# Token attention in a four-layer DiT: contraction in 128+128+32 channels, one transpose of maxima per unit, outputs packed to 96 rows, denominators per sequence

## The chip, the core and the metric

The kernel runs on one core of a Trainium2 chip. TensorE (PE) multiplies, VectorE (DVE), ScalarE (ACT) and GpSimd (POOL) work beside it, and SyncE (SP) issues nearly all DMAs, in the order of the program. The metric is the device time of one execution in microseconds; lower is better. All arithmetic is in float32.

## The reference

Four transformer blocks with adaptive layer norm are applied in turn to x, 4 sequences of 512 tokens with 288 channels. Each block is

```
mod  = silu(c) @ w_ada + b_ada                 # six vectors of 288 per sequence
h    = layernorm(x) * (1 + scale) + shift
q,k,v = split(h @ w_qkv + b_qkv)               # 16 heads of 18 channels
o    = softmax(q k^T / sqrt(18)) v
x    = x + gate * (o @ w_proj + b_proj)
h    = layernorm(x) * (1 + scale2) + shift2
x    = x + gate2 * mlp(h)                      # 288 -> 1152 -> 288, gelu
```

In layers 0, 1 and 3 the softmax runs over the 512 tokens of a sequence ("token attention"). In layer 2 it runs over the 16 heads of one token. Layer 0 has four experts in place of the MLP, two of them for each token. Biases are not zero.

## The kernel before

**Units and steps.** A token attention is cut into 16 units: 4 sequences times 4 groups of 4 heads. A unit has 4 steps, one for 128 tokens each, so there are 64 steps. `steps` (L729) writes the order out by hand. In step s the kernel computes, for four heads on four row groups of PE (32 rows each), the scores of the unit that is six steps ahead, only for their maxima over keys (`score`, L608; reduction on DVE, L660), and the scores of the current unit with the maxima already in them, transposed, so that ACT's exponential (L653) gives the weights at once. Two heads of each kind go in the first half of the step (`scores(step, 0)`), two in the second. Between the halves stands `sum_values` (L682): the weights of the step before, times values, summed into one PSUM bank over the unit's four steps. A column of ones among the values gives the denominator as a 19th row of each head.

**Two gaps.** After the sums and after the second half there is a `gap`: the place where other work is put in. Its argument is a number of microseconds by the program's own price list: `PACE = (0.3, 1.0)` (L526). Work is kept in four lists, sorted by the step in which each item is due: `products` (work for PE), `lanes` (norms and other chains), `loads` and `spreads` (DMAs). In a gap, an item is taken when what it reads is marked ready (`mark`, `ready`: counts of gaps, not times); with a budget of zero only items already due are taken. An item in `spreads` that yields WAIT keeps the list to itself until a later gap.

**Channels.** `chunks` (L486) turns the normed tokens, with channels on partitions, in three chunks of 96; the last has a 97th row of ones that carries the bias. `product` (L551) therefore needs three products for each output: `values(b, t)` four outputs of 128 x 288 per sequence, `queries_keys(b, m)` five outputs of 128 x 512 (the heads' queries and keys packed at 19 columns a head, 608 in all). Each result goes from its bank (6 or 7 in turn, `other`) to SBUF: L565 on DVE, L580 on ACT.

**Spread.** `spread(u)` (L598) copies the unit's queries and keys by 8 or more DMAs to one of four buffers `qk`, with 32 partitions for each head. It may run when the unit four earlier has used its buffer.

**Maxima.** `set_maxima(u)` (L664) turns the maxima, 128 x 4 for each of four token blocks, with four transposes (L668), copies 4 x 512 (L670), and writes each head's row into `qk` by a DMA (L672).

**Outputs.** Per unit, `denominators` (L693) turns the 128 x 512 sums with four transposes (L696), takes the reciprocals (L698), spreads them over 32 columns a head on POOL (L702); `normalise` (L706) turns them back with four transposes (L709) and multiplies on DVE (L712). `project` (L716, L719) multiplies four tiles of 128 rows, in which 18 rows of each 32 hold an output, with projection weights laid out the same way, for 128 tokens at a time; `add_gated` (L515, L516) adds the result to x.

**Around.** `load_attention` (L228) loads the weights by 32 small DMAs and two for the values; `scale_queries` (L272) scales the queries' weights on POOL. After a token attention come the expert blocks (layer 0) or the MLP, whose products have gaps of their own. The MLP for the first sequence of layer 1 runs inside the token attention, at step 48 (`early_mlp`). The MLP (`mlp`, L1575) already takes its channels as 128+128+32, the 32 of three outputs side by side in different rows of PE. Tiles live in pools with a fixed number of buffers by tag: `ot` has 7, `qc` 3, `rows` 1, `upd` 2.

Of the kernel before, what the change touches and what calls it, by code (L numbers as in the profile page):

```python
# [35 lines left out]
KF = 2  # L36
# [6 lines left out]
NQB = -(-NQ // P)  # L43
LEAD = 6
# [14 lines left out]
def tile_dit_blocks(ctx: ExitStack, tc: tile.TileContext, x_in, cond_t, sel_den, sel_b, w_gate, layers, out):  # L59
# [151 lines left out]
    mxs = [const.tile([P, TB, HG], F32, name=f"mx{i}") for i in range(2)]  # L211
# [16 lines left out]
    def load_attention(l):  # L228

        w, t = layers[l], w_att[l]  # L230

        wqk = wpool.tile([P, NK, NQ + C], F32, tag="wqk", name=f"wqk{l}")
        if l == OVER_HEADS:
# [3 lines left out]
        else:  # L237

            src = w["wqk"].rearrange("(k p) s (h d) -> p k s h d", p=KP, d=HP)
            bias = w["bqk"].rearrange("(o j d) s g -> o s g j d", o=1, d=HP)  # L240
            t["wqk"] = wqk[:, :, :NQ]
            wv = t["wv"] = wqk[:, :, NQ:]
            for g in range(NG):
                for s in range(2):
                    at = slice(g * UQ + s * HG * HO, g * UQ + (s + 1) * HG * HO)
                    for k in range(NK):
                        nc.sync.dma_start(
                            wqk[:KP, k, at].rearrange("p (j d) -> p j d", d=HO),
                            src[:, k, s, g * HG : (g + 1) * HG, :HO],
                        )  # L250
                    nc.sync.dma_start(
                        wqk[KP : KP + 1, NK - 1, at].rearrange("p (j d) -> p j d", d=HO), bias[:, s, g, :, :HO]
                    )
                if g == 0:
                    nc.sync.dma_start(wv[:KP], w["wv"].rearrange("(k p) f -> p k f", p=KP))
                    nc.sync.dma_start(wv[KP : KP + 1, NK - 1, :], w["bv"])
        mark(("loaded", l), 6)
        yield 0.0

    def load_projection(l):  # L260
        w, t = layers[l], w_att[l]
        wp = wpool.tile([P, NG, C], F32, tag="wp", name=f"wp{l}")
        t["wp"] = wp
        if l == OVER_HEADS:
            nc.sync.dma_start(wp[:KP, :NK, :], w["wp"].rearrange("(k p) f -> p k f", p=KP))
            nc.sync.dma_start(wp[KP : KP + 1, NK - 1, :], w["bp"])
        else:
            nc.sync.dma_start(wp, w["wp"].rearrange("(g p) f -> p g f", p=P))
# [3 lines left out]
    def scale_queries(l):  # L272

        for k in range(NK):
            n = KP + (1 if k == NK - 1 else 0)
            q = w_att[l]["wqk"][:n, k, :].rearrange("p (g s c) -> p g s c", g=NG, s=2)[:, :, 0, :]
            nc.gpsimd.tensor_scalar_mul(q, q, SCALE)
        mark(("weights", l))
        yield 0.2
# [61 lines left out]
    def mod_product(l, half, kinds):  # L341
# [13 lines left out]
        for kind in kinds:  # L355
            at = slice(kind * HP, kind * HP + B)
            nc.vector.tensor_tensor(row[at, :C], pr[at, :C], bada[at, :], ALU.add)
            if kind < 2 and half == 1 and l:
# [8 lines left out]
    def modulation(l, half, kinds=range(3)):  # L367
# [6 lines left out]
        if half == 0:  # L374
# [5 lines left out]
        if half == 0:  # L380
# [48 lines left out]
    def norm(l, half, b):  # L429
# [46 lines left out]
        elif half == 1:  # L476
# [9 lines left out]
    def chunks(l, half, b):  # L486
# [7 lines left out]
        for k in range(NK):  # L494
            if half == 0:
# [26 lines left out]
    def attention(l, start):  # L522
# [3 lines left out]
        PACE = (0.3, 1.0)  # L526
        qk, sums, done, ex, rec = {}, {}, {}, {}, {}
# [23 lines left out]
        def product(to, st, mv, us):  # L551

            for k in range(NK):
                rows = slice(0, KP + (1 if k == NK - 1 else 0))
                nc.tensor.matmul(to, st(rows, k), mv(rows, k), start=k == 0, stop=k == NK - 1)  # L555
                if k < NK - 1:
                    yield us

        def values(b, t):
            pv = other()[:, :C]  # L560
            h = ht[l, 0, b]
            yield from product(
                pv, lambda r, k: h[r, k, t * P : (t + 1) * P], lambda r, k: w["wv"][r, k, :], 0.48
            )
            nc.vector.tensor_copy(heads(vas[0])[:, t, :, :HD], pv.rearrange("p (h d) -> p h d", d=HD))  # L565
            count(b)
            yield 0.48

        packed = {}

        def queries_keys(b, m):

            h = ht[l, 0, b]
            n = min(P, NQ - m * P)
            pq = other()
            yield from product(
                pq[:n, :], lambda r, k: w["wqk"][r, k, m * P : m * P + n], lambda r, k: h[r, k, :], 0.86
            )
            t = packed[b, m] = work.tile([P, S], F32, tag="qc", bufs=3, name=f"qc_{l}_{b}_{m}")
            nc.scalar.copy(t[:n, :], pq[:n, :])  # L580
            mark(("packed", l, b, m), 1)
            count(b)
            yield 0.86
# [30 lines left out]
        def only_maxima(step):  # L614
# [7 lines left out]
            for j in range(HG):  # L622
                nc.vector.tensor_reduce(mxs[u % 2][:, c, j : j + 1], pm[j], AX.X, ALU.max)
# [16 lines left out]
        def scores(step, half):  # L640
# [16 lines left out]
            if maxima:  # L657
                for j in range(2):
                    h = 2 * half + j
                    nc.vector.tensor_reduce(mxs[mu % 2][:, mc, h : h + 1], pm[j], AX.X, ALU.max)  # L660
# [3 lines left out]
        def set_maxima(u):  # L664

            pm = other()
            for c in range(TB):
                nc.tensor.transpose(pm[:HG, c * P : (c + 1) * P], mxs[u % 2][:, c], ident)  # L668
            t = work.tile([P, S], F32, tag="qc", bufs=3, name=f"maxima_{l}_{u}")
            nc.scalar.copy(t[:HG, :], pm[:HG, :])  # L670
            for j in range(HG):
                nc.sync.dma_start(qk[u][j * HP + ONE : j * HP + ONE + 1, 0, :], t[j : j + 1, :])  # L672
            yield 0.5
# [19 lines left out]
        def denominators(u):  # L693
            pd = other()
            for c in range(TB):
                nc.tensor.transpose(pd[:, c * P : (c + 1) * P], done[u][:, c * P : (c + 1) * P], ident)  # L696
            r1 = small.tile([P, TB, HG, 1], F32, tag="r1", name=f"r1_{l}_{u}")
            nc.vector.reciprocal(  # L698
# [1228 lines left out]
```

## Time and profile before

| | |
|---|---|
| time, median of 3 runs | 2484.43 us (2483.38 to 2485.16) |
| the profiled execution, its span | 2486.91 us, 2485.2 us |
| token attention of layer 0, from the first score to the last copy of sums | 62 to 482 us |
| expert blocks | 488 to 928 us |
| token attention of layer 1 (with the early MLP) | 929 to 1369 us |
| MLP of layer 1, layer 2 | to 1945 us |
| token attention of layer 3 | 1946 to 2314 us |
| MLP of layer 3 | to 2485 us |
| TensorE's granted clock, mean | 0.943 |

How to read the profile: a row gives the line of the kernel, the engine, the operation, the tiles written and read, their shapes, and how often; then busy time, the mean of one instruction, and the idle time ahead of it with what ended it. A float32 product is two MATMUL rows. Products are pipelined, so the time that one takes from PE is read from the starts of two neighbours and not from its duration. In order of time, each row gives its start and length, both in us, and how many instructions were merged. The rows of a stretch give the busy us of PE, of its weight loads, of DVE, ACT and POOL, each with a count, then PE's granted clock, the share of the DMA engines and GB/s.

### The profile page before, as it was taken

The page shows a single profiled execution, that of the slowest core. Times are in us where ns is not written, and L with a number is a line of the kernel's source. Part 1 is how long each engine was busy: PE and PEld are TensorE (multiplying, and loading weights), DVE is VectorE, ACT ScalarE, POOL GpSimd, SP SyncE. Part 2 cuts the span into 40 slices and gives each one's busy share as a digit, 9 for nine tenths or more (in the row PEclk, how much of TensorE's full clock was granted, in tenths as well). Part 3 has the DMA queues.
Part 4 walks back from the last instruction along what each step waited for, and adds up shares of the span by engine and source line. Part 5 has one row for each costly group of instructions (what it writes and reads, how often), then busy time and mean ns, then how long its engine had stood idle before and what let it go on. Part 6 is the DMA issues. An engine that isn't in the chain of part 4 may idle for free. (4 is left out here: it accounts for less than half of the span.)

```text
span 2485.2 us, 30140 instructions
## 1 busy us (share of the span) xinstructions
PE 2291.2 (92%) x11188; PEld 1218.6 (49%) x11188; DVE 1086.3 (44%) x1955; ACT 834.8 (34%) x1233; POOL 521.4 (21%) x517
## 2 busy tenths in 40 slices
PE   5899999899998999999999999778589999999998
PEld 2333333367776773333353677455456433333455
DVE  2445655441012025555524669989210455555100
ACT  1244434422221223344426233323223244444311
POOL 2000020321022111100010257778621100011000
PEclk9699999999999997899999899888799799999999
DMA  5201110446554541000000001100110000000000
GB/s 143 97 30 62 38 36 12 107 161 189 177 160 152 175 124 62 13 14 16 28 21 1 22 3 32 36 17 17 22 56 2 28 16 16 14 14 6 1 20 20
DMA packets 163033, 134.23 MB, mean 54 GB/s; under 512 B 81365, under 2 KB 146725, under 8 KB 162886
## 3 DMA queue, kind: packets, MB, share of 16 engines
q1 hardware_dynamic: 159814, 122.86, 17.0%
q0 software_dynamic: 3072, 9.44, 1.2%
q8 instruction: 89, 1.46, 0.2%
q14 instruction: 58, 0.48, 0.1%
HBM read 90.67 MB, written 26.25 MB: 47 GB/s over the span
## 5 line engine op out<-in xcount | busy, mean ns | idle before, releaser
L660 DVE TENSOR_REDUCE mx<-banks 128x1 f32<-128x512 f32 x696 | 447.8, 685 | 370.9 <-PE banks L608 370.3
L608 PE MATMUL banks<-qk 32*128 32x512 f32 x3072 | 548.8, 681 | 11.8 <-DVE mx L660 7.0
L653 ACT ACTIVATE ex<-banks 128x1024 f32<-128x1024 f32 x348 | 356.4, 1024 | 513.2 <-PE banks L608 511.9
L608 PEld LDWEIGHTS banks<-qk 32*128 32x128 f32 x3072 | 180.5, 194 | 230.6 <-DVE mx L660 97.7
L863 POOL TENSOR_TENSOR pv<-hs,qk 128x1152 f32<-128x1152 f32 x64 | 203.7, 3196 | 50.2 <-DVE ho L875 35.3
L682 PE MATMUL banks<-ex,va 128*32 128x512 f32 x1536 | 212.2, 623 | 0.0
L1462 PE MATMUL banks<-w_b,hid_b 128*128 128x288 f32 x684 | 187.6, 417 | 0.0
L555 PE MATMUL banks<-ht,wqk 96*128 96x512 f32 (+1 forms) x360 | 186.7, 629 | 0.6 <-DVE upd_a L515 0.6
L1650 PE MATMUL banks<-ht,w 128*128 128x256 f32 x504 | 134.3, 402 | 38.2 <-ACT hid L1661 37.6
L1442 PE MATMUL banks<-block,w_b 128*128 128x256 f32 x684 | 165.8, 387 | 3.6 <-DMA w_b<-in_w 2.9
L702 POOL COPY rec<-r 128x512 f32<-128x512 f32 x48 | 29.6, 616 | 659.9 <-DVE r L698 586.2
L1672 PE MATMUL banks<-w,hid 128*128 128x288 f32 x504 | 151.8, 437 | 0.0
L1454 ACT ACTIVATE hid_b<-banks,b_b 128x256 f32<-128x256 f32 x171 | 68.7, 473 | 241.1 <-PE banks L1448 163.1
L1462 PEld LDWEIGHTS banks<-w_b,hid_b 128*128 128x128 f32 x684 | 123.9, 191 | 49.9 <-issue 21.9
L1442 PEld LDWEIGHTS banks<-block,w_b 128*128 128x128 f32 x684 | 129.3, 193 | 31.2 <-issue 11.4
L1650 PEld LDWEIGHTS banks<-ht,w 128*128 128x128 f32 x504 | 98.8, 201 | 61.7 <-ACT hid L1661 41.9
L719 PE MATMUL banks<-wp,ot 128*128 128x288 f32 x384 | 118.9, 435 | 5.9 <-DVE upd_a L515 3.5
L1672 PEld LDWEIGHTS banks<-w,hid 128*128 128x128 f32 x504 | 93.4, 198 | 46.3 <-issue 26.3
L516 POOL TENSOR_TENSOR x<-x,upd_a 128x288 f32<-128x288 f32 x48 | 38.1, 793 | 364.6 <-DVE upd_a L515 337.1
L555 PEld LDWEIGHTS banks<-ht,wqk 96*128 96x128 f32 (+1 forms) x360 | 61.4, 189 | 100.1 <-issue 86.2
L719 PEld LDWEIGHTS banks<-wp,ot 128*128 128x128 f32 x384 | 68.6, 195 | 76.1 <-issue 51.9
L682 PEld LDWEIGHTS banks<-ex,va 128*32 128x32 f32 x1536 | 31.1, 109 | 152.4 <-issue 150.6
(224 smaller groups left out, 2574.9 us busy)
## 6 DMA issues: line engine op xcount, KB each, us to landing
w_b<-in_w SPq DMA_DIRECT2D x57, 432.0 KB
w_b<-in_w SPq DMA_DIRECT2D x57, 384.0 KB
qk<-qc SPq DMA_DIRECT2D x336, 38.0 KB
wa<-in_wada SPq DMA_DIRECT2D x7, 864.0 KB
block<-x_mem SPq DMA_DIRECT2D x19, 288.0 KB
y_mem<-y_b SPq DMA_DIRECT2D x19, 288.0 KB
x_mem<-zeros SPq DMA_DIRECT2D x7, 768.0 KB
y_mem<-zeros SPq DMA_DIRECT2D x7, 768.0 KB
```

Source lines behind the costliest of these rows:

```text
L555: nc.tensor.matmul(to, st(rows, k), mv(rows, k), start=k == 0, stop=k == NK - 1)
L608: nc.tensor.matmul(to, qk[u][r, of, c * P : (c + 1) * P], qk[u][r, 1 - of, :], start=True, stop=True)
L653: nc.scalar.activation(e, WEIGHTS, AF.Exp)
L660: nc.vector.tensor_reduce(mxs[mu % 2][:, mc, h : h + 1], pm[j], AX.X, ALU.max)
L682: nc.tensor.matmul(SUMS[j * HP : (j + 1) * HP, :], vas[0][:, c, at : at + HP], ex[step, j // 2][:, j % 2, :], start=c == 0, stop=c == TB - 1,)
L719: nc.tensor.matmul(pp, done[b * NG + g][:, t * P : (t + 1) * P], w["wp"][:, g, :], start=g == 0, stop=g == NG - 1)
L863: nc.gpsimd.tensor_tensor(prod, sc[i][:, hs, :].unsqueeze(2).to_broadcast([P, GH, HD, NH]), qkv[i][:, 1].rearrange("p h d -> p d h").unsqu ...
L1442: nc.tensor.matmul(banks[:, UP + j, :BT], w1[:, k, j * P : (j + 1) * P], hx[i][:, k, :], start=k == 0, stop=False)
L1454: nc.scalar.activation(t, banks[:, UP + j, :BT], AF.Gelu_apprx_tanh, bias=b1[:, f : f + 1])
L1462: nc.tensor.matmul(banks[:, PY + t, :C], hid[j][:, t * P : (t + 1) * P], w2[:, j, :], start=f == 0, stop=f == NF - 1)
L1650: nc.tensor.matmul(banks[:, UP + j, :BT], full[:, k, (f % 3) * P : (f % 3 + 1) * P], h[:, k, s], start=k == 0, stop=False,)
L1672: nc.tensor.matmul(banks[:, PY + t, :C], hf[:, t * P : (t + 1) * P], w["w2"][f // 3][:, f % 3, :], start=False, stop=f == NF - 1,)
```

## The change

The token attentions of layers 0, 1 and 3 take channels as 128+128+32. The last 32 channels are held two more times below (32 to 63, 64 to 95), and two outputs are computed together (`products_of`), so that their remainders run side by side in different rows of PE; both outputs hold a bank until the end. Row 64 of the third weight chunk keeps the biases; at the start of a layer they are turned to columns and spread over partitions (`spread_biases`) and are added when a bank is emptied. The maxima are stored by head and block, so that one transpose of 16 columns does for a unit. When a unit's sums are copied, DMAs pack its heads, 18 rows each, into three tiles with 96 rows a sequence, and the denominators into 16 rows of the last (`gather_heads`). Once in a sequence the denominators are turned, inverted and turned back, written to memory, and read back over 18 rows a head by DMAs, in two groups; POOL multiplies. The projection takes three tiles. The first gap's budget is zero. The early MLP takes its hidden chunks in pairs.

```diff
-    mxs = [const.tile([P, TB, HG], F32, name=f"mx{i}") for i in range(2)]
+    mxs = [const.tile([P, HG, TB], F32, name=f"mx{i}") for i in range(2)]
...
     def load_attention(l):
...
+            chunk = [(k * P, P, 0, k) for k in range(KF)] + [(KF * P, RC, i * RC, KF) for i in range(2)]
             for g in range(NG):
                 for s in range(2):
-                    for k in range(NK):
+                    for c0, n, r0, k in chunk:
                         nc.sync.dma_start(
...
     def load_projection(l):
...
-            nc.sync.dma_start(wp, w["wp"].rearrange("(g p) f -> p g f", p=P))
+            for h in range(NH):
+                for k, r, at, n in parts_of(h):
+                    nc.sync.dma_start(wp[r : r + n, k, :], w["wp"][h * HP + at : h * HP + at + n, :])
+            nc.sync.dma_start(wp[KP : KP + 1, NK - 1, :], w["wp"][ONE : ONE + 1, :])
...
+    def spread_biases(l):
+        t = w_att[l]
+        row = t["all"][BIAS : BIAS + 1, KF, :]
+        pb = other()
+        for m in range(NQB):
+            n = min(P, NQ - m * P)
+            nc.tensor.transpose(pb[:n, m : m + 1], row[:, m * P : m * P + n], ident[BIAS : BIAS + 1, BIAS : BIAS + 1])
...
+        nc.tensor.matmul(pb, ones[BIAS : BIAS + 1, :], row[:, NQ:], start=True, stop=True)
+        t["bv"] = wpool.tile([P, C], F32, tag="bv", name=f"bv{l}")
+        nc.scalar.copy(t["bv"], pb)
...
-        PACE = (0.3, 1.0)
+        PACE = (0.0, 1.0)
...
+        def products_of(b, *which):
+            h = ht[l, 0, b]
+            jobs = []
+            for kind, i in which:
+                bank = other()
...
+            for kind, i, bank, product in jobs:
+                for k in range(KF):
+                    product(slice(0, P), k, k == 0, False)
+                    yield 0.48 if kind == "t" else 0.86
+            for j, (kind, i, bank, product) in enumerate(jobs):
+                product(slice(j * RC, (j + 1) * RC), KF, False, True)
...
         def set_maxima(u):
             pm = other()
-            for c in range(TB):
-                nc.tensor.transpose(pm[:HG, c * P : (c + 1) * P], mxs[u % 2][:, c], ident)
-            t = work.tile([P, S], F32, tag="qc", bufs=3, name=f"maxima_{l}_{u}")
-            nc.scalar.copy(t[:HG, :], pm[:HG, :])
+            n = HG * TB
+            nc.tensor.transpose(pm[:n, :P], mxs[u % 2].rearrange("p j c -> p (j c)"), ident)
+            t = small.tile([HG * TB, P], F32, tag="tops", bufs=1, name=f"tops_{l}_{u}")
+            nc.scalar.copy(t, pm[:n, :P])
...
-        def denominators(u):
...
+        def gather_heads(u):
+            b, g = divmod(u, NG)
...
+            for j in range(HG):
+                h = g * HG + j
+                for k, r, at, n in parts_of(h):
+                    nc.sync.dma_start(oc[b][k][r : r + n, :], done[u][j * HP + at : j * HP + at + n, :])
+                nc.sync.dma_start(last[KP + 1 + h : KP + 2 + h, :], done[u][j * HP + ONE : j * HP + ONE + 1, :])
+            mark(("packed heads", l, u), 2)
+            yield 0.0
+        def reciprocals(b):
+            pd = other()
+            rows = slice(KP, P)
+            for c in range(TB):
+                nc.tensor.transpose(
+                    pd[:, c * HP : (c + 1) * HP], oc[b][NK - 1][rows, c * P : (c + 1) * P], ident[rows, rows]
+                )
+            r1 = rec[b] = small.tile([P, TB, HP], F32, tag="r1", bufs=1, name=f"r1_{l}_{b}")
+            nc.vector.reciprocal(r1, pd[:, :P].rearrange("p (c h) -> p c h", c=TB))
+            mark(("reciprocals", l, b), 1)
+            yield 0.5
+        def reciprocal_rows(b):
...
+            nc.scalar.copy(t, pd[:HP, :])
+            mark(("reciprocal rows", l, b), 0)
...
-        def normalise(u):
+        def normalise(b):
+            rows = dram.tile([HP, S], F32, tag="rec", name=f"rec_rows_{l}_{b}")
+            nc.sync.dma_start(rows, rec[b])
+            room = {}
+            for ks in ((0, 1), (2,)):
+                t = work.tile([P, TB, C + 1], F32, tag="rows", bufs=1, name=f"by_{l}_{b}_{ks[0]}")
...
+                            nc.sync.dma_start(
+                                room[k][r : r + n, :], rows[1 + h : 2 + h, :].to_broadcast([n, S])
+                            )
+                for _ in range(3):
+                    yield WAIT
+                for k in ks:
+                    nc.gpsimd.tensor_tensor(oc[b][k][:KP, :], oc[b][k][:KP, :], room[k][:KP, :], ALU.mult)
+            mark(("outputs", l, b), 2)
+            yield 0.0
...
-                    products, at_step(last if b + 1 == B else last + (7 if l == 0 else 11) + t),
+                    products, at_step(last + 5 + t), [("outputs", l, b), ("gate", l, 0), ("projection", l)], project(b, t)
...
-                task(products, at_step(s + TB + 3), [("sums", l, u)], denominators(u))
-                task(products, at_step(s + TB + 5), [("reciprocals", l, u)], normalise(u))
+                free = [("x", l, 1, b - 1)] if b and not g else [("packed heads", l, u - 1)] if u else []
+                task(spreads, at_step(s + TB + 1), [("sums", l, u)] + free, gather_heads(u))
+            task(products, at_step(last + 2), [("packed heads", l, b * NG + NG - 1)], reciprocals(b))
+            task(products, at_step(last + 3), [("reciprocals", l, b)], reciprocal_rows(b))
+            task(spreads, at_step(last + 3), [("reciprocal rows", l, b)], normalise(b))
...
-        mlp(1, 0, b, TRIOS, home="hm")
+        mlp(1, 0, b, DUOS, home="hm")
```

## The prediction, on record before the result was known

> **What bounds the kernel now.** I read the page first, then the busy times by stretch, then PE's instructions in order of time inside the third token attention, where the clock is steady, then the DMA queue of SP.
>
> ```profile
> PE 2291.2 (92%) x11188; PEld 1218.6 (49%) x11188; DVE 1086.3 (44%) x1955; ACT 834.8 (34%) x1233; POOL 521.4 (21%) x517
> ...
> 2100.00:2200.00 100.00, 97.28 (x585) 34.99 (x588) 55.19 (x100) 47.47 (x55) 7.61 (x11) 1.00 0.05 16
> ```
>
> PE is busy 97.3 of 100 us there, DVE 55 and ACT 47: PE sets the pace, so fewer PE instructions should shorten the stage. Two stretches of the same layer show how far. First two full steps, then steps with no other product between the scores:
>
> ```profile
> 2157.32 1.14 PE L608 MATMUL banks<-qk 32*128 32x512 f32 x8
> 2158.39 1.06 PE L682 MATMUL banks<-ex,va 128*32 128x512 f32 x8
> 2159.38 1.12 PE L555 MATMUL banks<-ht,wqk 96*128 96x512 f32 x2
> 2160.44 1.14 PE L608 MATMUL banks<-qk 32*128 32x512 f32 x8
> 2161.51 1.99 PE L555 MATMUL banks<-ht,wqk 96*128 96x512 f32 x4
> 2163.43 1.14 PE L608 MATMUL banks<-qk 32*128 32x512 f32 x8
> 2164.50 1.06 PE L682 MATMUL banks<-ex,va 128*32 128x512 f32 x8
> 2165.49 0.66 PE L709 MATMUL banks<-ident,rec 128*128 128x128 f32 x4
> ...
> 2002.47 1.07 PE L682 MATMUL banks<-ex,va 128*32 128x512 f32 x8
> 2003.46 3.71 PE L608 MATMUL banks<-qk 32*128 32x512 f32 x16
> 2007.10 1.07 PE L682 MATMUL banks<-ex,va 128*32 128x512 f32 x8
> ```
>
> Start to start, one step is scores 1.07, sums 0.99, scores 1.07: 3.13 us of PE. The rest is products in two gaps: after the sums, and after the second scores. But the empty step takes 2007.10 - 2002.47 = 4.63 us: its two scores in a row need 3.64 instead of 2.14, because the second must wait for ACT's exponentials (1.02 us each) and DVE's maxima. So **the second gap holds 1.5 us of products for nothing**; what is removed below that returns nothing, although PE looks busy throughout. The ACT copies of the sums (L690) start at 1990.90 and, seven units later, at 2148.65: 22.5 us a unit of four steps, 90 a sequence of four units. 16 x 3.13 = 50 plus the 38 us of products of which I count the parts below agrees.
>
> **What the change removes from PE, per sequence.** An instruction below is one row of the trace; a float32 product is two of them, a transpose one.
> - Queries and keys: four instructions in 1.92 us (2161.51 to 2163.43), so 0.96 for a product. 15 become 13 (two pairs of 4 and one shared remainder; one of 3): -1.9. The remainder's two products run in different rows: three such took 17.0/15 = 1.13 us in the MLP (L1594), so 0.15 dearer than one: -1.6.
> - Values: L555 with 288 columns, 6 instructions in 1.65, 0.55 a product; 12 become 10: -1.1, with remainders -0.8.
> - Projection, same 0.55: 16 become 12: -2.2.
> - Transposes: 48 (maxima 16, sums 16, reciprocals 16) become 12; four take 0.6 (2165.49 to the next): 36 x 0.15 = -5.4.
>
> Together -10.0 us, times 12 sequences **-120 us**. It also takes 3.3 us of DVE work per sequence away (L712 688 ns, L698) and the POOL copies (616 ns); neither engine is late, so nothing is counted.
>
> **What comes back.** The order follows from due steps, so I placed the remaining 28 us of products per sequence step by step (second gap of step 0 for the values, 8 to 10 and 12 to 13 for the next queries and keys, 6 and 7 for the projection).
> - *Unfilled gaps.* About a third of the second gaps then hold under 1.5 us: 3 us lost per sequence in layer 3, also the short waits for both banks that a pair holds (evacuations L580 585 ns, L565 455 ns). Nine inner sequences: **+27** (bounds 0 to 45). In the last sequence of a layer no later products fill, and units there are 19.8, 16.7, 12.0 us already: 4.3 of the 10.0 is lost, **+13** (5 to 25).
> - *The wait for gathered rows.* The first reciprocal's transposes stand two gaps after the gather is issued. SP issues the spread of a later unit (9 DMAs, 588 ns each) just before, as its buffer comes free one step earlier; the gather is 8 DMAs.
>
> ```profile
> 2158.03 2.44 SPq L672 DMA_DIRECT2D qk<-maxima  x4
> 2167.31 7.59 SPq L598 DMA_DIRECT2D qk<-qc  x9
> 2180.62 2.43 SPq L672 DMA_DIRECT2D qk<-maxima  x4
> ```
>
>  6 us, then 8 x 0.56 = 4.5, then 1 to landing: 11.5 us after the sequence's end, while PE gets there after two steps, 9.3. That is 2.2; where the earlier gap is filled, 0.7. I take 1.3: nine times, **+12** (0 to 30). Behind PE's wait stand the next scores, so ACT and DVE wait too.
> - *Clock after a wait.* Around a wait for a DMA in layer 0 the granted clock fell:
>
> ```profile
> 410.00:425.00 15.00, 14.55 (x58) 5.52 (x50) 6.19 (x19) 4.73 (x7) 0.00 (x0) 0.66 0.07 20
> ```
>
>  15 us at 0.66 cost 5 us. With some such waits new, **+5** (0 to 25). The Trainium skill, "TensorE: Matmul & The Clock Gate", section "Why this matters for your kernels", asks for no idle gap over about 3 us; by it my shorter waits cost no clock and the sum would be 5 us better. The row above, where PE's shown wait was 0.45 us, speaks against leaving the term out.
> - *Ends of the three layers.* After the last step nothing hides the path: gather 4.5 + 1, copies, write of the reciprocals 0.36 plus about 2 to landing, 12 broadcasts, POOL's two products of 512 columns (L863 gives 2.77 ns a column: 1.4 each), 6 more broadcasts, one more product. A broadcast lies between L332 (272 ns) and L598 (588): I take 0.35, the row L1401 that also repeats a row of memory. That is 6 + 16 us against gaps of about 1.1 us (layers 0 and 1) or 2 us (layer 3) of MLP products, two and eight of them: PE waits about 8, 8 and 4, **+20** (6 to 45).
> - *Start and small things.* Layer 0 starts late by the 11 more weight DMAs (L247 477 ns, L255 321): 5 us, and first scores wait for SP today (18 spreads from 44.85 to 61.4, scores at 61.69); with the longer projection load and the pair's later evacuation 7. Spreading the biases 1.3 us a layer, MLP pairs instead of trios two remainders: **+13** (5 to 25).
>
> Sum: -120 + 27 + 13 + 12 + 5 + 20 + 13 = **-30 us**. The profiled execution took 2486.9 (span 2485.2 and 1.7 around it), so 2457; the median shown lies 2.5 below it: **2454 us**. With the bounds of the terms, all at once, -104 to +75; terms are independent, so I call 2425 to 2479 this case's own range.
>
> **Rivals.**
> - *Slower: SP's queue decides.* Per sequence SP issues 36 spreads and 16 maxima, 33.8 us by such spans (4 x (6.0, as most units have it, + 2.44)). Added are 34 gathers, 18 broadcasts and a write: 19.2 + 4.9 to 10.6 + 0.4. So 58 to 64 us of an 80 us sequence, in order, with waits for landing (2 us) and for POOL's 2.8 in it. Behind those stand the next maxima; today their last issue ends 8.6 us before their unit (2160.47 to the scores at 2169.06), and a gather and the broadcasts together are 9 to 12. From 0.6 us of wait per unit (30/48) on, the gain is gone; at 1.1 us the time is 2486.9 - 30 + 53 - 2.5 = 2507. For it: one queue at 75%, two long runs a sequence. Against: the maxima are known three steps before they are needed. The Trainium skill, "DMA: Bandwidth & Descriptors", section "Rules for kernel authors", says transfers under 64 KB pay mostly overhead; at the about 2 us it fits per DMA (another path), 53 would be an estimated 106 us a sequence and this case certain, but here four take 2.43.
> - *Much faster: everything is hidden.* If waits, clock and layer ends cost their lower bounds, -120 + 0 + 5 + 0 + 0 + 6 + 5 = -104; half way to it from -30, -67: 2417. For it: DVE and ACT are half idle. Against: the 4.63 us step.
> - *No change:* the terms cancel within 5 us, 0.2%, about what a measurement of this kernel can tell from no change.
>
> **Chances.** The forecast 0.42; much faster 0.14; no change 0.09; slower 0.35. So faster 0.56, same 0.09, slower 0.35. The range 2400 to 2515 leaves out half of the much faster case and a third of the slower one, 0.19.
>
> **What would show it.** PE instructions fall by about 4 x 3 x (4 + 4 + 8 + 36), 620, less some biases. Unit distances in layer 3 go from 22.5 to about 21.6 us: at 20 the much faster case holds, at 23 SP. New rows would be PE's waits for the gathered tile and for outputs, together 12 + 20 us; a wait of L608 for maxima over 30 us (1.0 today) would show SP deciding. I am wrong most easily in the place of the remaining products, which I derived from due steps and not from an order I could see.

## The result, and the profile after

The changed kernel takes **2654.12 us** (median of 4 runs, 2652.55 to 2663.76); the kernel before, run beside it, 2483.9 us. The ratio is 1.0696, 95% interval 1.0672 to 1.0721: 7% slower. The forecast was 2454, the range 2400 to 2515. Of the cases written down, the rival in which SP's queue decides comes nearest; it gave 2507.

The page's first row, then the stretch of layer 3 that was shown of the kernel before, and short stretches inside and just after it; in these rows the granted clock stands third from the end:

```profile
PE 2302.6 (87%) x10681; PEld 1218.6 (46%) x10681; DVE 1057.6 (40%) x1886; ACT 828.2 (31%) x1248; POOL 547.7 (21%) x517
```

```profile
2100.00:2200.00 100.00, 90.99 (x463) 30.27 (x460) 47.12 (x75) 41.34 (x47) 0.00 (x0) 0.89 0.07 20
2200.00:2208.00 8.00, 6.89 (x27) 1.89 (x27) 2.25 (x3) 1.28 (x2) 0.00 (x0) 0.50 0.01 3
2208.00:2212.00 4.00, 4.00 (x20) 1.30 (x20) 1.29 (x2) 1.02 (x1) 0.00 (x0) 0.98 0.00 0
2244.00:2251.00 7.00, 6.88 (x21) 2.15 (x22) 0.35 (x1) 1.83 (x3) 0.00 (x0) 0.50 0.07 20
2254.00:2260.00 6.00, 6.00 (x32) 3.14 (x29) 3.04 (x5) 2.93 (x4) 0.55 (x1) 1.00 0.09 22
```

PE has 507 instructions fewer, and is busy longer (2302.6 against 2291.2 us). It is busy 91 of 100 us where it was 97, and the clock is at half speed in two short stretches. PE's waits, each with its total in us, the number of times and the longest one:

```profile
PE banks L765 <- DMA oc<-ot: 52.6, 10, 8.4
PE banks L1514 <- DMA block<-x_mem: 41.8, 3, 22.2
...
PE banks L654 <- DMA qk<-tops: 35.1, 10, 7.6
```

L765 is the transpose of the gathered denominators, L654 the scores (L608 before), L1514 a block of the MoE layer. In the kernel before, the wait for the block was 4.3 us and that for the maxima 1.0; the first had no counterpart. Two of these waits, PE's instructions in order of time, a few rows each (idle time and its end in brackets):

```profile
2200.37 0.60 PE L765 MATMUL banks<-ident,oc 32*128 32x32 f32 x4 [5.56 <-DMA oc<-ot]
2200.91 0.38 PE L714 MATMUL banks<-ident,mx 128*16 128x128 f32 x1
2202.03 2.08 PE L605 MATMUL banks<-ht,wqk 128*128 128x512 f32 x2 [0.74 <-DVE r L769]
2204.03 2.09 PE L654 MATMUL banks<-qk 32*128 32x512 f32 x8
2206.05 1.94 PE L731 MATMUL banks<-ex,va 128*32 128x512 f32 x8
...
2212.05 1.07 PE L731 MATMUL banks<-ex,va 128*32 128x512 f32 x8
```

```profile
2244.12 2.63 PE L654 MATMUL banks<-qk 32*128 32x512 f32 x4 [7.43 <-DMA qk<-tops]
```

After the wait of 5.56 us the same eight products of the sums take 1.94 us, and 1.07 six microseconds later. So such a wait is paid twice: once itself, and once in the half clock behind it. SP's queue around them:

```profile
2184.28 5.84 SPq L644 DMA_DIRECT2D qk<-qc  x9
2190.42 0.77 SPq L756 DMA_DIRECT2D oc<-ot  x1
...
2198.37 0.54 SPq L757 DMA_DIRECT2D oc<-ot  x1
...
2223.60 0.37 SPq L786 DMA_DIRECT2D rec_rows<-rec  x1
2231.55 9.06 SPq L796 DMA_DIRECT2D by<-rec_rows  x18
2240.65 2.96 SPq L718 DMA_DIRECT2D qk<-tops  x4
```

The gather's eight DMAs (L756, L757) stand behind a spread and take 8.5 us to issue, not 4.5. The maxima of the next unit (L718) stand behind 18 broadcasts; the scores that need them wait 7.43 us.

Where the 166.8 us between the two spans lie, by the starts of the copies of the sums (a unit's end; L690 before, L739 after), in us:

| stage | before | after | products alone (e1) | outputs alone (e2) |
|---|---|---|---|---|
| start, to the first unit's end | 129.3 | 149.6 | 149.8 | 135.3 |
| the three token attentions, first to last unit's end | 1071.2 | 1161.0 | 1076.3 | 1155.2 |
| between layers 0 and 1 | 490.2 | 523.4 | 510.5 | 489.4 |
| between layers 1 and 3 | 622.8 | 643.3 | 634.9 | 631.5 |
| after the last unit | 171.8 | 174.7 | 171.8 | 175.3 |
| half clock in all | 285 | 521 | 347 | 435 |

"Half clock" is the time in which the trace's record of the granted clock says 0.5. 236 us more of it can cost up to 118 of the 167 us.

### The profile page after: what moved, and what is told of

It is laid out like the page before. It is cut to its first block, busy times and chain, and to the rows that moved or that the text cites. A ratio compares the mean times of both kernels' runs of the same rounds, so it can differ in the third digit from the quotient of the medians.

```text
span 2652.0 us, 29951 instructions
## 1 busy us (share of the span) xinstructions
PE 2302.6 (87%) x10681; PEld 1218.6 (46%) x10681; DVE 1057.6 (40%) x1886; ACT 828.2 (31%) x1248; POOL 547.7 (21%) x517
## 5 line engine op out<-in xcount | busy, mean ns | idle before, releaser
L654 PE MATMUL banks<-qk 32*128 32x512 f32 x3072 | 658.0, 704 | 56.3 <-DMA qk<-tops 35.1
L654 PEld LDWEIGHTS banks<-qk 32*128 32x128 f32 x3072 | 244.1, 201 | 380.3 <-issue 167.9
L731 PE MATMUL banks<-ex,va 128*32 128x512 f32 x1536 | 227.0, 661 | 0.0
L802 POOL TENSOR_TENSOR oc<-oc,by 96x512 f32<-96x512 f32 x36 | 45.4, 1261 | 860.4 <-DMA by<-rec_rows 859.4
L605 PE MATMUL banks<-ht,wqk 128*128 128x512 f32 (+1 forms) x360 | 170.6, 653 | 5.3 <-DVE r L769 3.7
L1561 PEld LDWEIGHTS banks<-w_b,hid_b 128*128 128x128 f32 x684 | 125.1, 192 | 49.7 <-issue 21.1
L1553 ACT ACTIVATE hid_b<-banks,b_b 128x256 f32<-128x256 f32 x171 | 69.1, 473 | 226.4 <-PE banks L1547 131.7
L1772 PEld LDWEIGHTS banks<-w,hid 128*128 128x128 f32 x504 | 93.0, 197 | 46.3 <-issue 26.1
L946 DVE TENSOR_TENSOR pq<-banks,qk 128x1152 f32<-128x1152 f32 x64 | 86.1, 1346 | 41.2 <-issue 21.8
L605 PEld LDWEIGHTS banks<-ht,wqk 128*128 128x128 f32 (+1 forms) x360 | 54.1, 194 | 91.4 <-issue 80.2
L473 DVE BATCH_NORM_STATS2 st<-x 128x6 f32<-128x288 f32 x128 | 56.2, 439 | 99.8 <-POOL x L1785 80.1
L952 DVE TENSOR_REDUCE hs<-pq 128x64 f32<-128x1152 f32 x64 | 86.6, 1353 | 14.5 <-POOL pv L962 11.7
```

What stands on the lines that cost most here:

```text
L605: nc.tensor.matmul(bank[:n, :], w["wqk"][r, k, i * P : i * P + n], h[r, k, :], start=start, stop=stop)
L654: nc.tensor.matmul(to, qk[u][r, of, c * P : (c + 1) * P], qk[u][r, 1 - of, :], start=True, stop=True)
L731: nc.tensor.matmul(SUMS[j * HP : (j + 1) * HP, :], vas[0][:, c, at : at + HP], ex[step, j // 2][:, j % 2, :], start=c == 0, stop=c == TB - 1,)
L946: nc.vector.tensor_tensor(prod, QUERIES[i % 2][:, :C].rearrange("p (h d) -> p h d", d=HD)[:, hs, :].unsqueeze(2).to_broadcast([P, GH, NH, ...
L952: nc.vector.tensor_reduce(sc[i][:, hs, :], prod, AX.X, ALU.add)
L1561: nc.tensor.matmul(banks[:, PY + t, :C], hid[j][:, t * P : (t + 1) * P], w2[:, j, :], start=f == 0, stop=f == NF - 1)
```

## The experiments

Ratios are to the kernel before, run beside it on the same chip. That took 2480 to 2493 us on these occasions, so runs are compared by their ratios: a difference of 0.01 between two ratios is 25 us of 2484. First the two halves of the change, and the issuing engine of two groups of DMAs.

**e1, the products' part.** The output path (`denominators`, `normalise`, `project`, `load_projection` and their tasks) is that of the kernel before.

> The changed kernel with the output path of the kernel before (denominators and products with them per unit, 128-row heads, the weights of the projection in one DMA); paired products, biases, the one transpose of maxima and the pace are the change's. Theory (SP's queue: gathers, write and broadcasts of the denominators stand in front of the maxima): without them SP has room again, the PE work of the products and of 12 maxima transposes per sequence, 4.2 us x 12 = 50 us, is gone and at most part of it comes back as empty gaps and a longer start: 2430 to 2480 us, the wait of the scores for the maxima under 3 us. Rival (the paired products, their two held banks or the empty first gap cost more than they save): over 2520 us.

2543.9 us, 1.0247 (1.0230 to 1.0264). The theory fails here: without the new DMAs there is still a loss of 2.5%. The wait for the maxima is 15.4 us, under half of that after the change but not under the 3 us expected. By the table the sequences gain nothing, and start and stages between the layers lose 53 us.

**e2, the outputs' part**, on the kernel before (`gather_heads`, `reciprocals`, `reciprocal_rows`, `normalise`, `project`, `load_projection` and their tasks).

> The kernel before with the change's output path alone (heads packed to 96 rows by gathers, denominators per sequence, broadcasts through DRAM, projection over three chunks); products, maxima and pace as before. Theory (SP's queue): as slow as the whole change or nearly so, 2570 to 2700 us, with waits of scores or reciprocals for DMAs of over 50 us in all and half-clock time over 400 us. Rival (the products are what costs): 2420 to 2500 us.

2590.36 us, 1.0440 (1.0422 to 1.0457): as expected of the queue. The two halves add up: 2.5% and 4.4% against 7.0%.

**e3, the output DMAs on GpSimd.**

```
-   nc.sync.dma_start(...)      # gather_heads, normalise
+   nc.gpsimd.dma_start(...)
```

> The changed kernel with the DMAs of its output path (gathers, write and broadcasts) issued from GpSimd instead of SyncE; nothing else. Theory (the order on SP's queue): spreads and maxima no longer stand behind the broadcasts that wait for GpSimd, 2420 to 2540 us, the wait for the maxima is under 5 us. If the gathers' number or their landing is what counts whoever issues them, or if GpSimd's own issue is dear: 2600 us or more, and the wait for the gathered rows stays.

2594.24 us, 1.0458 (1.0439 to 1.0477): 59 us less than the change by the ratios, a third of the loss, and less than the theory said. PE's waits:

```profile
PE banks L765 <- DMA oc<-ot: 22.5, 8, 5.3
PE banks L810 <- POOL oc L802: 15.1, 5, 5.9
```

The wait for the gathered rows is under half, the one for the maxima 4.1 us, and a new one for GpSimd's products has come.

**e4, the maxima's DMAs on ScalarE**: `nc.sync` becomes `nc.scalar` in `set_maxima`.

> The changed kernel with the four DMAs of the maxima issued from ScalarE, behind the copy that makes them; nothing else. If the late maxima are the main part of the loss (35 us of waits shown and the half clock that follows each): 2560 to 2610 us. If the gathered rows or the spreads are: 2630 to 2660 us. If the issue on ScalarE delays the exponentials (32 issues per layer and sequence group at about 0.5 us): over 2660 us.

2775.54 us, 1.1177 (1.1155 to 1.1199), the third case. ScalarE's waits:

```profile
ACT ex L699 <- DMA qk<-tops: 162.1, 32, 11.9
```

The DMA may only be issued when the spread below it has landed. SP waited for that; now ScalarE does, once seen for 4.1 us and then 2.5 us for four issues, and the exponentials stand behind it. Which engine issues is a question of who may wait.

**e5, the pace alone**, PACE (0.0, 1.0) in the kernel before.

> The kernel before with the change's pace (0.0 us of products in the first gap of a step instead of 0.3); nothing else. In the first run of this study the products' part gained nothing in the sequences, although its products and transposes of maxima are 4.2 us of PE work per sequence less: its groups of four scores were 78 us longer in all than in the kernel before, where a group without work since the exponential of the one before takes 1.4 to 1.8 us instead of 1.14. Theory (the empty first gap stretches the score groups and opens waits): this kernel is slower, 2500 to 2550 us. Rival (the pace is harmless, the pairs are what stretches): 2470 to 2495 us.

2485.34 us, 1.0011 (0.9996 to 1.0027): harmless.

**e6, e1 with the old pace.**

> The products' part alone (as in the first run) with the pace of the kernel before, 0.3 us in the first gap. If the empty first gap is what ate its gain: 2470 to 2515 us (the gain of up to 50 us in the sequences against some 50 us of longer start and longer stages between the layers). If the pairs and their two held banks ate it: 2530 to 2560 us, as with the change's pace.

2532.34 us, 1.0214 (1.0187 to 1.0242), whose interval overlaps that of e1. The pace is not the cause.

**e7, the maxima alone**: the store by head and block, one transpose, one short copy, in the kernel before.

> The kernel before with the change's handling of the maxima alone: one transpose of 16 columns per unit instead of four of 4, one copy of 128 instead of 512 columns. 3 transposes of 0.15 us for each of 48 units are 22 us of PE work. If what is taken from PE in the sequences is gained: 2455 to 2475 us. If it comes back as longer score groups or empty gaps: 2475 to 2490 us.

2483.55 us, 1.0012 (0.9994 to 1.0030). 144 transposes less, and nothing gained. Some 12 of the 22 us come back in one wait of PE, shown before and in this run:

```profile
PE banks L668 <- DVE mx L660: 15.8, 19, 1.9
```

```profile
PE banks L668 <- DVE mx L660: 27.5, 24, 2.7
```

The one transpose needs the last maximum of VectorE. Of the four, three did not, and filled PE's time until it came. Another form of the loss, in order of time:

```profile
2070.14 1.07 PE L685 MATMUL banks<-ex,va 128*32 128x512 f32 x8
2071.14 0.28 PE L668 MATMUL banks<-ident,mx 128*16 128x128 f32 x1
2071.34 1.25 PE L608 MATMUL banks<-qk 32*128 32x512 f32 x8
```

The transpose stands in the first gap, and the scores behind it take 1.25 us instead of 1.14. Two of its four products begin 0.12 us after the other two, so a group of scores that comes too early does not wait as a whole: some of it begins, the rest follows, and the group is longer. PE looks busy meanwhile.

**e8, no wait for GpSimd on SP**: the memset on VectorE, the third chunk's broadcasts in a buffer of their own.

```
-   nc.gpsimd.memset(last[KP:, :], 1.0)
+   nc.vector.memset(last[KP:, :], 1.0)
...
-   t = work.tile([P, TB, C + 1], F32, tag="rows", bufs=1, ...)   # for ks == (2,)
+   t = work.tile([P, 2, C], F32, tag="upd", bufs=2, ...)
```

> The changed kernel without SyncE's two waits for GpSimd in the output path: the ones under the denominators are set by VectorE instead of GpSimd, and the broadcast rows of the third chunk go to a buffer of their own (that of the updates), so that their DMAs need not wait for the product of the first two. The number of DMAs is unchanged. If the waits in the queue make the maxima late: 2590 to 2625 us, with the scores' wait for the maxima (35 us) under 12 us. If the mere issue of 52 DMAs per sequence does: 2640 to 2665 us and the wait stays over 25 us.

2658.15 us, 1.0717 (1.0689 to 1.0745): nothing. SP still waits for the memset:

```profile
SPq L757 <- DVE oc L752: 82.5, 8, 24.4
```

In the changed kernel SP's rows were

```profile
SPq L757 <- POOL oc L752: 69.9, 8, 25.7
SPq L756 <- DMA qk<-qc: 46.3, 59, 1.1
```

So only the other wait was really taken out, which was 11.8 us in all (the broadcasts' wait for GpSimd's products). PE's wait for the maxima fell from 35.1 to 22.5 us, and the time did not follow. That speaks against the late maxima as the main part.

**e9, e6 with the first spreads on GpSimd.** In the products' part the pairs make several packed tiles ready at once. SP in e6, and PE's wait that comes of it:

```profile
761.04 20.35 SPq L641 DMA_DIRECT2D qk<-qc  x18
...
783.29 11.49 SPq L641 DMA_DIRECT2D qk<-qc  x9
795.96 0.66 SPq L1426 DMA_DIRECT2D block<-x_mem  x1
```

```profile
805.49 1.08 PE L1469 MATMUL banks<-ident,block 128*128 128x128 f32 x4 [22.02 <-DMA block<-x_mem]
```

```
+   queue = nc.gpsimd if u < 3 else nc.sync      # in spread(u)
```

> The products' part alone with the old pace, with the 27 DMAs that spread the queries and keys of the first three units of each layer issued from GpSimd instead of SyncE. In that kernel the pairs make several packed tiles ready at once, so that these DMAs stand back to back on SyncE: 27 from 58.6 us at the start (18 in the kernel before, from 44.9), and between layers 0 and 1 they stand ahead of a load of a block, for which PE then waits 22.0 us (4.3 before). Theory (the bunched spreads on the one queue are what the start and the stages between the layers lose): the 22 us wait falls under 6 us, the stage between the first two attention layers goes from 503 back to 490 us or less, in all 2505 to 2520 us. Rival (the spreads come late because the paired products end late, whoever issues them): 2525 to 2540 us.

2499.2 us, 1.0028 (1.0013 to 1.0044), better than the theory said. The block's wait is 6.4 us, the start 133.1, the stage between layers 0 and 1 495.1. By the ratios this takes off 46 of the 53 us that e6 had lost; part of that the kernel before would gain too (e18).

**e10, e11: which of the output DMAs.** Write and broadcasts alone, then gathers alone, on GpSimd.

> The changed kernel with the write and the 18 broadcasts of the reciprocals per sequence issued from GpSimd; the 34 gathers stay on SyncE. With gathers and broadcasts on GpSimd it took 2594 us, with both on SyncE 2654. If the broadcasts (which also wait for the write's landing, 3.7 us per sequence, and for GpSimd) are what delays the maxima: 2590 to 2615 us, and the scores' wait for the maxima falls from 35 to under 8 us. If the gathers are: 2640 to 2660 us.

2632.47 us, 1.0551 (1.0525 to 1.0576); the maxima wait falls to 12.0, the one for the gathered rows stays at 53.0.

> The changed kernel with the 34 gathers per sequence issued from GpSimd; write and broadcasts stay on SyncE. If the gathers' 34 issues at 0.54 to 0.73 us (21 us of SyncE per sequence) are what delays spreads, maxima and the reciprocals: 2590 to 2620 us, and PE's wait for the gathered rows (52.6 us in all) falls under 25 us. If the broadcasts are: 2635 to 2660 us. If both share it, both of these runs lie near 2625 us.

2615.57 us, 1.0497 (1.0472 to 1.0522); the wait for the gathered rows falls to 21.2, that for the maxima is 27.3. Both share it, the gathers more: by the ratios 36 us for write and broadcasts, 49 for the gathers, and 59 for both together (e3), so the two overlap.

**e12, the denominators' transposes later.**

```
+   mark(("gathered", l, u), 6)                  # after mark(("packed heads", l, u), 2)
-   ... [("packed heads", l, b * NG + NG - 1)], reciprocals(b))
+   ... [("gathered", l, b * NG + NG - 1)], reciprocals(b))
```

> The changed kernel with the transposes of the denominators due two steps later, so that the gathered rows have landed before PE comes to them; all that follows them moves too. In the changed kernel PE waits 52.6 us in ten of the twelve sequences there, at the prediction's 1.3 us each it would have been 12, and the clock is halved after most of these waits. If this wait and the half clock behind it are a main part: 2560 to 2610 us, with over 60 us less of half clock. If the same delay only turns up at another wait (maxima, projection): 2635 to 2665 us.

2570.51 us, 1.0303 (1.0279 to 1.0327): by the ratios 98 us, over half of the whole loss, from two steps of delay; half clock 98 us less. PE's longest waits are now

```profile
PE banks L714 <- DVE mx L706: 40.8, 33, 4.7
...
PE banks L654 <- DMA qk<-tops: 25.9, 6, 12.7
PE banks L1515 <- DMA block<-x_mem: 25.9, 2, 20.8
```

and the row of the gathered denominators is gone from the largest ones.

**e13, all of it mended**: e12, the output DMAs and the first three spreads of a layer on GpSimd, the old pace.

> The changed kernel with everything that the runs showed to be at fault mended: gathers, write and broadcasts and the spreads of the first three units of a layer issued from GpSimd, the transposes of the denominators two steps later, the old pace. Alone, these took 60 us (output DMAs), 84 us (later transposes), 33 us (first spreads, in the products' part) and 12 us (pace, there) off. If they are separate causes: 2465 to 2490 us. If they overlap (the same wait moved twice): 2495 to 2550 us. If removed PE work is gained once the queue is out of the way: under 2460 us.

2534.81 us, 1.0171 (1.0146 to 1.0195): the causes overlap. A new wait is the largest:

```profile
PE banks L812 <- POOL oc L804: 61.3, 10, 11.1
```

**e14, e15, e16: what sets a step when PE has less to do.** The first edit leaves out half of the keys from the maxima (e14 in e13's kernel, e16 in the kernel before), the second half of the exponentials (e15, in e13's kernel; those weights stay at 1).

```
-   pm[j], AX.X, ALU.max)                 +   pm[j][:, : S // 2], AX.X, ALU.max)
-   nc.scalar.activation(e, WEIGHTS, AF.Exp)
+   nc.scalar.activation(e[:, :, : S // 2], WEIGHTS[:, :, : S // 2], AF.Exp)
```

> The mended kernel with the maxima of the full steps taken over 256 of the 512 columns (so the maxima are those of half the keys): VectorE's part of a step falls from some 2.6 us to some 1.4 us, PE's work is the same. Theory (VectorE's maxima, which release the three score banks, set the step, so that removed PE work turns into waits): 30 us or more under the mended kernel. Rival (the exponential, which releases the one pair of score banks, sets it): within 12 us of it.

2516.66 us, 1.0110 (1.0072 to 1.0148), 18 us under the mended kernel.

> The mended kernel with the exponentials of the full steps taken over 256 of the 512 columns (the other half stays at 1.0, set once per layer by GpSimd): ScalarE's part of a step falls from 2.05 us to some 1.2 us, PE's work is the same. Theory (VectorE's maxima set the step): within 12 us of the mended kernel. Rival (the exponential sets it): 30 us or more under it.

2514.49 us, 1.0083 (1.0057 to 1.0108), 20 us under it.

> The kernel before with the maxima of the full steps taken over 256 of the 512 columns (maxima of half the keys). If VectorE sets the step in the kernel before already, and PE's 95% busy is in part waiting that shows as longer score groups: 30 us or more under the kernel before. If PE's own work sets it there: within 12 us.

2475.64 us, 0.9934 (0.9908 to 0.9960). None meets its numbers: halving one engine's work gives a little each time, in the kernel before too. The traces tell two things apart. PE's wait of the maxima's transpose for VectorE is 29.1 us in e13 and 14.4 in e14, 15.8 in the kernel before and 5.7 in e16. And where no product stands between two groups of scores, rows of e13, e14 and e15 are

```profile
2074.09 3.66 PE L655 MATMUL banks<-qk 32*128 32x512 f32 x16
```

```profile
2062.83 3.66 PE L655 MATMUL banks<-qk 32*128 32x512 f32 x16
```

```profile
2062.89 3.14 PE L655 MATMUL banks<-qk 32*128 32x512 f32 x16
```

From the start to PE's next instruction, at full clock and from the first to the last unit's end of the three attentions, such a pair takes 3.6 us on average in e13 (36 pairs), 3.6 in e14 (40) and 3.1 in e15 (36). So half the exponentials shorten an empty step, and half the maxima do not. For the filled steps it stays open; both halved together was not tried.

**e17, e13 with the projection two steps later**: `mark(("outputs", l, b), 2)` becomes 6.

> The mended kernel with the projection due two steps later as well. In the mended kernel PE waits 61.3 us in ten of the twelve sequences for GpSimd's products before the projection, where the change itself had 1.5: the delay of the transposes and the longer issue on GpSimd came out there. If that wait is the rest of the loss: 2535 less 61, and less up to some 30 us of half clock behind it: 2445 to 2485 us, faster than the kernel before. If the steps have a floor that PE's work does not set, so that the wait is filled but nothing is gained: 2485 to 2520 us.

2522.01 us, 1.0162 (1.0137 to 1.0186), which cannot be told from e13's ratio: the case in which the wait is filled and nothing is gained. The 61.3 us wait is gone from PE's list; in its place stand

```profile
PE banks L655 <- ACT ex L700: 27.3, 13, 4.5
...
PE banks L1516 <- DMA block<-x_mem: 23.3, 2, 16.8
```

**e18, the first spreads on GpSimd in the kernel before**, the edit of e9.

> The kernel before with the spreads of the first three units of each layer issued from GpSimd. In the products' part this took 33 us off, because 27 DMAs stood back to back on SyncE there; in the kernel before they come in 9s and 18s (44.9 to 61.4, 69.6 to 89.4 us) and one load of a block is late by 4.3 us. If the queue delays the start there too: 2470 to 2485 us against some 2490. If only the pairs make them bunch: within 4 us of the kernel before.

2467.82 us, 0.9938 (0.9921 to 0.9955): faster than both kernels. Start 120.8 instead of 129.3 us, between layers 0 and 1 484.9 instead of 490.2; layer 3 unchanged, 322.6. So SP's queue held up the start without pairs too, and the same edit was worth more in the products' part (46 us against 15). With it in both kernels the products' part (e9) is still 0.9% slower, some 22 us, which no run here takes apart.

## Why the prediction was wrong

The work that the change removes was estimated well; what removing it buys was not, nor what the new DMAs cost. Forecast was -30 us; the ratio of 1.0696 is +173, and that of e17, with later due times and a second queue, +40. So of the 203 us between forecast and result some 133 go when DMAs are out of PE's way, with the half clock behind the waits, and some 70 stay: in the main removed work that did not come out as time. For 15 units of layer 3, from the first unit's end to the last, each moment of PE put to the function whose instruction runs, to the earlier one where two do (us; the transposes of the normed channels, 6.2 to 6.7 in each column, are left out):

| | before | maxima alone (e7) | products, old pace (e6) | after | mended (e17) |
|---|---|---|---|---|---|
| whole stretch | 322.6 | 324.9 | 327.1 | 352.1 | 329.2 |
| products of queries, keys, values | 59.8 | 60.6 | 49.7 | 51.8 | 48.9 |
| projection | 28.8 | 28.5 | 28.7 | 18.5 | 21.0 |
| maxima's transposes | 7.9 | 3.4 | 3.7 | 3.8 | 3.7 |
| denominators, reciprocals | 16.4 | 16.3 | 17.7 | 3.4 | 2.3 |
| scores | 132.1 | 131.7 | 136.3 | 165.8 | 162.1 |
| sums | 60.0 | 61.5 | 61.9 | 65.6 | 63.3 |
| idle | 11.1 | 16.4 | 22.7 | 36.8 | 21.1 |
| half clock within it | 0 | 3.4 | 6.8 | 51.2 | 20.5 |

- *The removal, -10.0 us per sequence.* From before to after the four rows of products, projection and transposes fall by 35.4 us in 3.75 sequences, 9.4 a sequence: right in size, though part of it ran at half clock. The count of instructions was wrong by 96 (507 fewer, not about 600): two remainders side by side are still two, only their time overlaps.
- *A step that failed: "Unfilled gaps", +27 and +13, a third of the removal.* Nearly all of the removal came back. In e17, where the long waits are gone, these rows are 37.0 us lower than before, scores and sums 33.3 higher, idle 10.0 higher; even with its half clock taken off (at most 10.3 us) only 3.7 us are gained. So 8.8 us a sequence came back in layer 3 (33.3 and 10.0, less 10.3, in 3.75 sequences), where 3 was priced. Empty second gaps, the term's own mechanism, are a part of it: pairs of score groups with nothing between are 4 in this stretch before, 10 after and 18 in e17, each some 1.5 us dearer than two covered groups, so 2.4 us a sequence after and 5.5 in e17. What the term left out is the filled steps: groups of eight at full clock take 1.12 us on average before, 1.31 after and 1.18 in e17 (idle time not counted), and PE idles longer. e7 shows it alone: 22 us of transposes for nothing. The prediction had the right sign of it, the step of 4.63 us with the group of 3.64 instead of 2.14, but read PE's 97% as a bound for the filled steps. Part of the work filled time that PE had to let pass: until the exponentials are done in an empty step (e15), until the last maximum is there before a transpose (e7, e14, e16). What sets a filled step stays open.
- *A step that failed: "The wait for gathered rows", 12 us (bounds 0 to 30).* 52.6 us are shown in ten waits: seven, 32.5 us, in the nine inner sequences that the term is for, three, 20.1 us, at the ends of the layers. The rows came about when the prediction said: in those seven the transposes begin 11.7 us (median) after the copy of the last sums begins, where 11.5 had been reckoned. The gather issues over 8.5 us and not 4.5, as by the profile SP waits in it for the landing of the spread's DMAs (59 waits at L756, 46.3 us in all), but it starts earlier. What was wrong is PE's place: it stood there after 7.2 us (median), not 9.3. Among the waits that the sum priced this is the one with the largest error, and giving the transposes two steps more took 98 us off (e12).
- *A term that was far too small: "Clock after a wait", 5 us (0 to 25).* 236 us more at half clock, up to 118 us. The row at 0.66 was read rightly, but priced for "some" waits; there are 48 stretches of half clock instead of 28.
- *The rival of SP's queue.* Its sign of 35.1 us waiting for maxima (over 30 was named) came true, and moving the output DMAs to another queue is worth 59 us. But it was priced at the maxima only. The maxima wait could be cut by 12.6 us for nothing (e8); the gathers on the same queue were worth more than write and broadcasts (e10, e11), and the spreads held up the start (e9). That the case came nearest is in part luck.
- *Start and layer ends, 33 us in all.* Start 20.3, between the layers 33.2 and 20.5, end 2.9: 77. The start was to come from more weight DMAs (they cost 3.2 us on SP, the last of wqk being issued until 29.2 instead of 26.0) and 7 us; its main part was not on the list: pairs finish several packed tiles at once, and their spreads fill SP for 27 us (e9 against e6 brought 16.3 of it back). The new ends of the layers were priced high enough: in e2, which has them without the pairs, the three stages behind an attention change by -0.8, +8.7 and +3.5 us, where 20 was taken. In e1, with the pairs and the old ends, they are 32.4 us longer.
- *The causes are not separate.* Alone, by the ratios, the later transposes were worth 98 us, the output DMAs 59, the first spreads 46 (in the products' part) and the pace at most 8; together 130 (e13). Each moved the wait to what comes next (e13, L812). What remains in e17, 1.6%, lies in the start (4.7 us), between the layers (9.3 and 11.5) and in the attentions (12.8); which waits make up the stages between the layers was not settled.

## What to carry to other kernels

A busy PE is a bound only where its groups are as short as they can be: compare one group's duration in filled and empty steps, and try the smallest piece of a removal alone before adding up the rest. On a queue that works in order, count what stands in front of the tight transfers for every stage, and ask what comes in bunches; the cure can be a second queue on an engine that may wait, not on one that answers PE. A wait of PE of a few microseconds was paid again in half clock here, so due times behind a new DMA are worth more slack than its mean latency.

## What the runs showed of the hardware

- The same 27 spreads took 26.8 us to issue on SP in e6 (58.1 to 84.9) and 14.1 us on GpSimd in e9, rows of which are

```profile
57.07 6.76 POOL L642 DMA_DIRECT2D qk<-qc  x13 [1.04 <-ACT qc L621]
66.07 7.33 POOL L642 DMA_DIRECT2D qk<-qc  x14 [2.25 <-ACT qc L621]
```

  0.52 us each. The Trainium skill, "DMA: Bandwidth & Descriptors", section "Issuing engines are not separate DMA queues", says that issuing on several engines saves only the sequencer's time, usually small beside the DMA itself; here moving DMAs to a second engine was worth 59 us of 2654 (e3) and 0.6% of the kernel before (e18).
- Idle time of PE and the clock: in eight of these profiles (before, after, e1, e2, e3, e12, e17, e18), of 55 gaps of 2 to 3 us that began at full clock 49 had half clock set in by 7 us after their end, and all 61 of 3 to 5 us, 83 of 96 longer ones; of 246 gaps of 0.8 to 2 us 62, no more than of those of 0.4 to 0.8 us (82 of 310). The limit of about 3 us that the prediction cites did not hold here: gaps of 2 to 3 us had half clock behind them too.
